# Second graph layer: all parts in float32r, one group's matrices copied by GpSimd, two groups' made by VectorE in one step

## The chip, the cores and the metric

The kernel runs on one core of a Trainium2 chip. The metric is device microseconds for one launch; the time before is the median of three runs. The engines are named as in the profile: PE (TensorE, with PEld for its weight loads), DVE (VectorE), ACT (ScalarE), POOL (GpSimd) and SP, which here only issues DMAs.

## The reference

Four graph layers on 3327 nodes with 512 features, each with a residual around it. Layers 0 to 2 are graph attention with 8, 4 and 8 heads, layer 3 averages neighbours. The change touches layer 1, which has four heads of 128 features:

```python
h = jnp.maximum(_layernorm(x, axis=-1), 0.0)
Wh = (h @ W).reshape(n, 4, 128)
sl = jnp.einsum('nhd,hd->nh', Wh, a_l)
sr = jnp.einsum('nhd,hd->nh', Wh, a_r)
e = leaky_relu(sl[:, :, None] + sr.T[None, :, :], 0.2)
e = where(adj + eye > 0, e, -inf)
alpha = softmax(e, axis=2)
x = x + elu(einsum('nhm,mhd->nhd', alpha, Wh))
```

The exponential of a leaky ReLU of a sum is a product on each side of the kink: where sl + sr > 0 it is exp(sl) exp(sr), elsewhere exp(0.2 sl) exp(0.2 sr). So the softmax sum for one head is two matrix products, one over the neighbours with sl + sr > 0 and one over the other neighbours, with 0/1-like matrices (the mask holds 2.0 for an edge; the factor cancels in the division) and the rows exp(sr) Wh and exp(0.2 sr) Wh, each with the factor itself as a 129th column.

## The kernel before

Nodes lie in 26 tiles of 128. Outputs are worked through in seven chunks (six of four tiles, one of two); sources are grouped as `JG`: three groups of six tiles (0 to 2) and two of four (3 and 4). In `attention`, for each chunk and head of layer 1, there are two halves (`a` = 0 for the positive side, 1 for the other), and for each half passes over pairs of output tiles. A pass runs all 26 source tiles for its two output tiles; both accumulators lie in PSUM (`acc`).

The weights of each matmul are a 128x128 block of the 0/1 matrix. `matrices` makes these in fp8 for all five groups: `compare` asks for sl + sr > 0 (L670 on ACT by a scaled ReLU, or L667 on DVE for the source tiles in `GP_ON_DVE[1]`, tiles 18 to 25, groups 3 and 4), then `split` ANDs the result with the mask as 32-bit words (L674). Between the two halves every matrix is turned into that of the other side in place, by XOR with the mask (L794).

The moving operand is the table `ab`, stored in DRAM per group and loaded again for each head and half (L714, from SP's queue, seven buffers). Its form is set by `KIND`, a letter for each group, "bssvv":

- group 0 ("b"): rows are cut into three bf16 pieces (`pieces`: 387 columns), and the fp8 matrix is itself the weights (L762).
- groups 1 and 2 ("s") and 3 and 4 ("v"): rows are cut into two float32r parts (`parts`: 258 columns), and the fp8 matrix is first copied into float32r for the two output tiles of a pass by `real` (L639): "s" by ACT into `ts` (three buffers), "v" by DVE into `tv` (two buffers). The matmul is L759.

After a pass DVE sums the pieces from PSUM into `R` (L780); after the second half of a head it scales and divides (L802 to L809). Finished chunks go to node stages of the next layer, spread over the following passes by `Hooks`: residual and ELU (L866 to L870, the add L869 on POOL), layer norm (L345 to L357, three small steps L350 to L352 on POOL), projection, scaling (L450) and the pieces for layer 2 (L387 to L397, where L395 is a subtraction on POOL). The order on each engine's queue is written by a scheduler from the program's order and the added order-only dependencies (`after`); each engine then works its queue in order.

The matrices lie in `tht` (ten buffers), the scores of the output tiles, broadcast over partitions, in `s1b` (two buffers, loaded at L682), the mask of a chunk in five `m` tiles out of six buffers (L271). The negated scores of the source tiles are in `L.ns2`, one value a partition for each tile and head.

Of the kernel before, what the change touches and what calls it, by code (L numbers as in the profile page):

```python
# [25 lines left out]
F32 = mybir.dt.float32  # L26
BF16 = mybir.dt.bfloat16
I32 = mybir.dt.int32
U32 = mybir.dt.uint32
FP8 = mybir.dt.float8e4  # L30
F32R = mybir.dt.float32r
# [6 lines left out]
P = 128  # L38
# [4 lines left out]
S2_MAX = 30.0  # L43
S_CLIP = 40.0

GP_ON_DVE = [(5, 12, 19), tuple(range(18, 26)), (4, 9, 14, 19, 24)]


KIND = "bssvv"


@with_exitstack
def tile_gnn(ctx: ExitStack, tc: tile.TileContext, x, adj, W0, a01, W1, al, ar, W2, a2,
# [60 lines left out]
    for l in range(3):  # L114
        H, DA, AO, HW = dims(l)
        if l == 1:
            abd.append([dram.tile([H, 2, P, nj, AO], BF16, name=f"ab{l}_{g}") if KIND[g] == "b" else
                        dram.tile([H, 2, P, nj, 2 * DA], F32, name=f"ab{l}_{g}") for g, (_, nj) in enumerate(JG)])
        else:
            abd.append([dram.tile([H, P, nj, HW], BF16, name=f"ab{l}_{g}") for g, (_, nj) in enumerate(JG)])  # L120
    y1d = [dram.tile([n * P, D], F32, name=f"y1_{c}") for c, (_, n) in enumerate(chunks)]
# [247 lines left out]
    def pieces(L, t, AB, pool, first, behind=None):  # L369

        l = L.l
        g, jj = jwhere[t]
        H, DA, AO, HW = dims(l)

        o, two = (t % 2, 2) if first else (0, 1)
        if o == 0:
            L.pt = pool.tile([P, H, 2, two, AO] if l == 1 else [P, H, two, HW], BF16, name="pt", bufs=3 if first else 2)
        pt = L.pt
        nc.gpsimd.memset(pt[:, :, :, o, 3 * DA:AO] if l == 1 else
                         pt[:, :, o].rearrange("p h (a w) -> p h a w", a=2)[..., 3 * DA:AO], 1.0)  # L380

        def dst(s, a):
            if l == 1:
                return pt[:, :, a, o, s * DA:(s + 1) * DA]
            return pt[:, :, o, a * AO + s * DA:a * AO + (s + 1) * DA]
        r = pool.tile([P, 2, H, DA], F32, name="r", bufs=2 if first else 1)
        sb = nc.vector.tensor_sub(r, AB, high(AB))  # L387
        if behind:
            after(sb, behind)
        for a in range(2):  # L390
            cp = nc.scalar.copy(dst(0, a), high(AB[:, a]))
            if behind:
                after(cp, behind)
        for a in range(2):
            nc.gpsimd.tensor_sub(dst(2, a), r[:, a], high(r[:, a]))  # L395
        for a in range(2):
            nc.scalar.copy(dst(1, a), high(r[:, a]))  # L397
        js = slice(jj + 1 - two, jj + 1)
        if o == two - 1 and l == 1:
            for a in range(2):  # L400
                L.to_store.append((abd[l][g][:, a, :, js, :].rearrange("h p j w -> p h j w"), pt[:, :, a]))
        elif first and o == two - 1:
            if g not in ahead:
                ahead[g] = pieces_tile(L, bp, g)
            nc.sync.dma_start(ahead[g][:, js], pt[:, 0])
            stored[t] = nc.sync.dma_start(abd[l][g][:, :, js, :].rearrange("h p j w -> p h j w"), pt).ins.name
        elif o == two - 1:
            L.to_store.append((abd[l][g][:, :, js, :].rearrange("h p j w -> p h j w"), pt))
# [46 lines left out]
    def parts(L, t, AB, pool, first, behind=None):  # L455

        l = L.l
        g, jj = jwhere[t]
        H, DA, AO, HW = dims(l)
        H2 = H // 2  # L460
        if l == 1 and KIND[g] != "b":
            for f in range(2):
                hs = slice(f * H2, (f + 1) * H2)
                pt = pool.tile([P, H2, 2, 2, DA], F32R, name="pt", bufs=2)
                v = pt.rearrange("p h a s d -> p s a h d")
                cp = nc.scalar.copy(v[:, 0], AB[:, :, hs])
                if behind:
                    after(cp, behind)
                nc.vector.tensor_sub(v[:, 1], AB[:, :, hs], v[:, 0].bitcast(F32))
                L.to_store.append((abd[l][g][hs, :, :, jj, :].rearrange("h a p w -> p h a w"),  # L470
                                   pt.rearrange("p h a s d -> p h a (s d)").bitcast(F32)))
        else:
            pieces(L, t, AB, pool, first, behind)
        if t == JG[g][0] + JG[g][1] - 1:
            js = slice(JG[g][0], t + 1)
            nc.vector.tensor_scalar(L.ks2[:, js], L.s12[:, 1, js, :], BIG, None, op0=ALU.mult)
            nc.vector.tensor_scalar(L.ns2[:, js], L.s12[:, 1, js, :], -1.0, None, op0=ALU.mult)
# [153 lines left out]
            while self.tiles or self.flying:  # L631
                self.run(1, 0, 0)

    def real(a, g, ks, th):

        nj = JG[g][1]
        k0, k1 = ks[0], ks[-1] + 1
        t = mp.tile([P, 2, nj, P], F32R, name="ts" if KIND[g] == "s" else "tv", bufs=3 if KIND[g] == "s" else 2)
        (nc.scalar.copy if KIND[g] == "s" else nc.vector.tensor_copy)(t[:, :k1 - k0, :nj], th[a][g][:, k0:k1])  # L639
        return t  # L640

    ahead = {}
# [42 lines left out]
    def attention(L, hooks, open_next, close):  # L685
# [5 lines left out]
        for c, (t0, nt) in enumerate(chunks):  # L691
# [3 lines left out]
            for h in range(H):  # L695
# [10 lines left out]
                for a in range(2 if l == 1 else 1):  # L706
                    row = []
                    for g, (_, nj) in enumerate(JG):
                        if l == 1:
                            tl = mp.tile([P, JM * 2 * DA], F32R, name="ab", bufs=7)  # L710
                            two = KIND[g] != "b"
                            w = 2 * DA if two else AO
                            v = (tl if two else tl.bitcast(BF16))[:, :nj * w].rearrange("p (j w) -> p j w", j=nj)
                            ld = nc.sync.dma_start(v.bitcast(F32) if two else v, abd[l][g][h, a])  # L714
                        else:
                            if g in ahead:
                                v = ahead.pop(g)
                            else:
                                v = pieces_tile(L, mp if l else bp, g)
                                ld = nc.sync.dma_start(v, abd[l][g][h])  # L720
                        row.append(v)
                    ab.append(row)
# [4 lines left out]
                for g in range(len(JG)):  # L727
                    if g in early:
                        pv, gv = early.pop(g)
                    else:  # L730

                        pt = mp.tile([P, PER * JM * P], FP8, name="tht", bufs=10 if l == 1 else 7)
                        gt = pt if l == 1 else mp.tile([P, PER * JM * P], FP8, name="gt", bufs=7)
                        pv, gv, words, steps = matrices(L, nt, h, g, s1v, masks[g], pt, gt)
                        for step in steps:
                            step()
                        if l == 1:
                            flip.append(words)
                    th[0].append(pv)
                    th[1].append(gv)  # L740
                R = mp.tile([P, PER, 2, DA], F32, name="R", bufs=1)
                deg = l == 0 and h == 0
                for a in range(2 if l == 1 else 1):
# [5 lines left out]
                    for ks, js in passes:  # L749
                        thr = {}  # L750
                        for j in js:
                            g, jj = jwhere[j]
                            if l == 1 and KIND[g] != "b" and g not in thr:
                                thr[g] = real(a, g, ks, th)
                            for k in ks:
                                if j == 0:
                                    acc[k] = accs.tile([P, 512], F32, name="acc")
                                if g in thr:
                                    mm = nc.tensor.matmul(acc[k][:, :2 * DA], thr[g][:, k - ks[0], jj, :], ab[a][g][:, jj, :],  # L759
                                                     start=(j == 0), stop=(j == NT - 1), skip_group_check=True)  # L760
                                elif l == 1:
                                    mm = nc.tensor.matmul(acc[k][:, :3 * DA], th[a][g][:, k, jj, :], ab[a][g][:, jj, :3 * DA],  # L762
                                                     start=(j == 0), stop=(j == NT - 1), skip_group_check=True)
                                else:
                                    o = 1 if deg else 0
# [11 lines left out]
                            continue  # L777
                        for k in ks:
                            if l == 1:
                                nc.vector.tensor_reduce(R[:, k, a, :], acc[k][:, :3 * DA].rearrange("p (s d) -> p d s", s=3),  # L780
                                                        AX.X, ALU.add)
                            else:
                                v = acc[k][:, :2 * AO].rearrange("p (a w) -> p a w", a=2)[:, :, :3 * DA]
                                nc.vector.tensor_reduce(R[:, k], v.rearrange("p a (s d) -> p a d s", s=3), AX.X, ALU.add)  # L784
# [113 lines left out]
    with tc.tile_pool(name="first", bufs=1) as fp:  # L898
# [47 lines left out]
        while hooks.small:  # L946
# [1 line left out]
    A, R = [("A", D, F32, n) for n in A_BUFS], ("R", PER * 2 * 129, F32, 1)  # L948
    ab, gt, tht = ("ab", JM * 400, BF16, 7), ("gt", PER * JM * P, FP8, 7), ("tht", PER * JM * P, FP8, 7)
    tags = [[A[0], ("R", PER * 2 * 65, F32, 1), tht, ("tr", JM * P, BF16, 5), ("abx", 4 * 400, BF16, 4), gt],  # L950
            [A[1], ("ab", JM * 258, F32R, 7), R, ("ts", 2 * JM * P, F32R, 3), ("tv", 2 * 4 * P, F32R, 2), tht[:3] + (10,)],
            [A[2], ab, ("R", PER * 2 * 65, F32, 1), tht, gt]]
    hooks.masks = in_steps([mask_steps(ip, t, g) for t, g in order[20:]])
    for l in range(3):
# [530 lines left out]
```

## Time and profile before

| What | Value |
|---|---|
| Median of three runs | 3552.45 us (3546.64 to 3554.89) |
| Profiled execution, span | 3551.1 us (no other time of this execution is listed) |
| PE busy | 3442.3 us, 97% of the span |
| DVE busy | 2624.3 us, 74% |
| ACT busy | 2507.0 us, 71% |
| POOL busy | 618.8 us, 17% |
| Layer 1, first to last aggregation matmul | 1233.3 to about 2072 us |
| Mean granted TensorE clock | 0.990 |

A row of the groups names the line, engine and operation, the tiles written and read, the shape of what is written and read, and the count; then busy time in all, mean nanoseconds of one, and the idle time of that engine just before, with what ended most of it. A row of the timeline gives the start, the length, and a run of equal instructions with its count. PE's rows of consecutive matmuls overlap, since their ends are modelled; starts are the safer reading.

### The profile page before, as it was taken

Reading aid. Unit: us, or ns where it says so; the run is one execution under the profiler, and the core shown is the slowest. Engines: PE = TensorE matmul, PEld = TensorE weight load, DVE = VectorE, ACT = ScalarE, POOL = GpSimd, SP = SyncE. Lnnn points to the kernel's source line nnn. Section 1 sums busy time; section 2 is a strip of 40 time slices with the busy share of each in tenths; the row PEclk is TensorE's granted clock in tenths of the full one; section 3 lists DMA queues with packets and bytes.
Section 4 is the critical chain, followed back from the end, with each engine's and each line's share of the span. In section 5 each row is a group of like instructions: output and inputs, shape, how many; then the busy total and the mean of one; then the engine's idle time right before and its main releaser. Section 6 shows DMA issues by size and latency. Waiting matters only on the chain. (4 is left out here: it accounts for less than half of the span.)

```text
span 3551.1 us, 77646 instructions
## 1 busy us (share of the span) xinstructions
PE 3442.3 (97%) x30751; PEld 3107.2 (88%) x30751; DVE 2624.3 (74%) x5227; ACT 2507.0 (71%) x4113; POOL 618.8 (17%) x858
## 2 busy tenths in 40 slices
PE   7899999999999999999999989999999999999998
PEld 6789999999999888888888869989898989876887
DVE  7788888888887699888888868867676768672121
ACT  5777787878787789888888677767666757572111
POOL 6611222112111202222223320101010101020000
PEclk9999999999999999999999999999999999999999
DMA  7699999999857787777777875555545555576331
GB/s 207 223 282 251 233 263 238 268 260 250 256 203 247 246 285 276 279 269 273 269 273 254 332 268 190 191 175 189 183 166 181 185 172 188 168 271 257 105 107 54
DMA packets 398120, 797.72 MB, mean 225 GB/s; under 512 B 112970, under 2 KB 221845, under 8 KB 397105
## 3 DMA queue, kind: packets, MB, share of 16 engines
q1 hardware_dynamic: 363890, 723.14, 63.4%
q0 software_dynamic: 28128, 62.42, 7.6%
q10 hardware_dynamic: 5726, 7.08, 0.6%
q8 instruction: 245, 4.01, 0.5%
q14 instruction: 131, 1.07, 0.1%
HBM read 663.59 MB, written 129.64 MB: 223 GB/s over the span
## 5 line engine op out<-in xcount | busy, mean ns | idle before, releaser
L670 ACT ACTIVATE gt<-s1b,ks 128x512 fp8e4<-128x512 f32 (+1 forms) x2448 | 1448.2, 677 | 276.4 <-issue 160.1
L766 PE MATMUL acc<-ab,tht 128*128 128x195 bf16 (+1 forms) x9112 | 1553.1, 248 | 5.4 <-DVE tht L674 4.6
L769 PE MATMUL acc<-ab,gt 128*128 128x195 bf16 (+1 forms) x9112 | 1552.2, 248 | 5.0 <-DVE rc L806 3.3
L769 PEld LDWEIGHTS <-gt 128*128 128x128 fp8e4 x10744 | 1053.6, 98 | 40.1 <-issue 27.4
L766 PEld LDWEIGHTS <-tht 128*128 128x128 fp8e4 x10744 | 1053.4, 98 | 24.8 <-DVE tht L674 11.5
L674 DVE TENSOR_TENSOR tht<-gt,m 128x768 uint32<-128x768 uint32 (+3 forms) x557 | 445.5, 800 | 129.4 <-ACT gt L670 125.5
L676 DVE TENSOR_TENSOR gt<-tht,m 128x768 uint32<-128x768 uint32 (+3 forms) x557 | 448.0, 805 | 8.7
L639 ACT CAST ts<-tht 128x1536 fp32r<-128x1536 fp8e4 x208 | 300.0, 1470 | 55.6 <-PE acc L759 52.5
L759 PE MATMUL acc<-ab,ts 128*128 128x258 f32 x2496 | 333.4, 289 | 4.7 <-ACT ts L639 3.4
L759 PEld LDWEIGHTS acc<-ab,ts 128*128 128x128 f32 x2496 | 313.2, 190 | 13.2 <-ACT ts L639 3.8
L667 DVE TENSOR_SCALAR gt<-s1b,ns 128x512 fp8e4<-128x512 f32 (+1 forms) x446 | 218.2, 495 | 129.4 <-PE acc L769 125.1
L1021 PE MATMUL acc<-y,mf 128*128 128x512 f32 x1352 | 309.8, 391 | 1.1 <-DVE mf L1016 1.1
L670 ACT ACTIVATE tht<-s1b,ks 128x512 fp8e4<-128x512 f32 (+1 forms) x504 | 308.4, 680 | 2.3 <-DMA s1b<-s 1.7
L1021 PEld LDWEIGHTS acc<-y,mf 128*128 128x128 f32 x1352 | 253.6, 188 | 57.2 <-DVE mf L1016 1.5
L769 PE MATMUL acc<-abx,gt 128*128 128x195 bf16 (+1 forms) x1632 | 287.4, 249 | 11.6 <-DVE rc L806 5.6
L766 PE MATMUL acc<-abx,tht 128*128 128x195 bf16 (+1 forms) x1632 | 287.8, 249 | 4.6 <-DVE tht L674 3.0
L869 POOL TENSOR_TENSOR xt<-xt,e 128x512 f32<-128x512 f32 x72 | 121.9, 1693 | 916.8 <-DVE e L868 583.9
L784 DVE TENSOR_REDUCE R<-acc 128x130 f32<-128x390 f32 x416 | 214.2, 554 | 79.5 <-PE acc L769 78.9
L762 PE MATMUL acc<-ab,tht 128*128 128x387 bf16 x1248 | 225.8, 329 | 8.9 <-DMA ab<-ab 5.8
L1018 ACT CAST mf<-m 128x768 fp32r<-128x768 fp8e4 (+1 forms) x78 | 59.1, 762 | 244.5 <-PE acc L1021 232.7
L759 PE MATMUL acc<-ab,tv 128*128 128x258 f32 x1664 | 218.8, 283 | 1.4 <-DVE tv L639 1.2
L759 PEld LDWEIGHTS acc<-ab,tv 128*128 128x128 f32 x1664 | 207.2, 189 | 2.9 <-DVE tv L639 2.1
(163 smaller groups left out, 3710.2 us busy)
## 6 DMA issues: line engine op xcount, KB each, us to landing
ab<-ab SPq DMA_DIRECT2D x333, 600.0 KB, 5.3
ab<-ab SPq DMA_DIRECT2D x112, 774.0 KB, 6.5
ab<-ab SPq DMA_DIRECT2D x112, 516.0 KB, 5.3
ab<-ab SPq DMA_DIRECT2D x112, 400.0 KB, 4.0
abx<-ab SPq DMA_DIRECT2D x110, 400.0 KB, 7.9
ab<-ab SPq DMA_DIRECT2D x56, 582.0 KB, 7.3
s1b<-s SPq DMA_DIRECT2D x120, 256.0 KB, 6.5
m<-mask SPq DMA_DIRECT2D x69, 384.0 KB, 4.4
```

The source lines that it names most:

```text
L639: (nc.scalar.copy if KIND[g] == "s" else nc.vector.tensor_copy)(t[:, :k1 - k0, :nj], th[a][g][:, k0:k1])
L667: nc.vector.tensor_scalar(gv[:, :, jj, :], s1v, L.ns2[:, j, h:h + 1], 2.0, op0=ALU.is_gt, op1=ALU.mult, saturate=False)
L670: nc.scalar.activation(gv[:, :, jj, :], s1v, AF.Relu, bias=L.ks2[:, j, h:h + 1], scale=BIG, saturate=False)
L674: nc.vector.tensor_tensor(pu, gu, mu, ALU.bitwise_and)
L676: nc.vector.tensor_tensor(gu, pu, mu, ALU.bitwise_xor)
L759: mm = nc.tensor.matmul(acc[k][:, :2 * DA], thr[g][:, k - ks[0], jj, :], ab[a][g][:, jj, :], start=(j == 0), stop=(j == NT - 1), skip_grou ...
L762: mm = nc.tensor.matmul(acc[k][:, :3 * DA], th[a][g][:, k, jj, :], ab[a][g][:, jj, :3 * DA], start=(j == 0), stop=(j == NT - 1), skip_grou ...
L766: nc.tensor.matmul(acc[k][:, :3 * DA + o], th[0][g][:, k, jj, :], ab[0][g][:, jj, :3 * DA + o], start=(j == 0), stop=False, skip_group_che ...
L769: mm = nc.tensor.matmul(acc[k][:, AO:AO + 3 * DA + o], th[1][g][:, k, jj, :], ab[0][g][:, jj, AO:AO + 3 * DA + o], start=False, stop=(j == ...
L784: nc.vector.tensor_reduce(R[:, k], v.rearrange("p a (s d) -> p a d s", s=3), AX.X, ALU.add)
L869: nc.gpsimd.tensor_add(xt, xt, e)
L1021: nc.tensor.matmul(acc[k], mf[:, jj, :], y2[g][:, jj, s, :], start=(j0 + jj == 0 and s == 0), stop=(j0 + jj == NT - 1 and s == 1))
```

## The change

`KIND` becomes "gssdd", and all five groups are stored and loaded as two float32r parts of 258 columns. What follows from the letters:

- group 0 ("g"): `real` copies its fp8 matrix into float32r with GpSimd (`tg`, two buffers), and the matmul is that of the other groups.
- groups 1 and 2 ("s"): unchanged.
- groups 3 and 4 ("d"): no fp8 matrix is made; there is no compare, AND, XOR or copy. For each pass and source tile, one DVE instruction compares the broadcast scores with the tile's negated score (greater for the first half, less or equal for the second), multiplies by the mask and writes float32r (`td`, two buffers).

`GP_ON_DVE[1]` is empty, since its tiles are those of groups 3 and 4. The reduce from PSUM sums two parts of 129. The `ab` tiles get two names, `ab6` (five buffers) and `ab4` (three), and `tht` goes from ten buffers to seven. The branches for group 0's bf16 pieces in `pieces`, `parts`, the tables in DRAM and the matmuls go.

```diff
-GP_ON_DVE = [(5, 12, 19), tuple(range(18, 26)), (4, 9, 14, 19, 24)]
+GP_ON_DVE = [(5, 12, 19), (), (4, 9, 14, 19, 24)]
-KIND = "bssvv"
+KIND = "gssdd"
+TD = 2
...
-        if l == 1 and KIND[g] != "b":
+        if l == 1:
             for f in range(2):
...
-    def real(a, g, ks, th):
+    def real(L, a, g, ks, th, h, s1v, mask):
-        nj = JG[g][1]
+        j0, nj = JG[g]
         k0, k1 = ks[0], ks[-1] + 1
-        t = mp.tile([P, 2, nj, P], F32R, name="ts" if KIND[g] == "s" else "tv", bufs=3 if KIND[g] == "s" else 2)
-        (nc.scalar.copy if KIND[g] == "s" else nc.vector.tensor_copy)(t[:, :k1 - k0, :nj], th[a][g][:, k0:k1])
+        if KIND[g] == "d":
+            t = mp.tile([P, 2, nj, P], F32R, name="td", bufs=TD)
+            for jj in range(nj):
+                nc.vector.scalar_tensor_tensor(t[:, :k1 - k0, jj, :], s1v[:, k0:k1, :], L.ns2[:, j0 + jj, h:h + 1],
+                                               mask[:, k0:k1, jj, :], op0=ALU.is_le if a else ALU.is_gt, op1=ALU.mult)
+            return t
+        copy = {"g": nc.gpsimd.tensor_copy, "s": nc.scalar.copy}[KIND[g]]
+        t = mp.tile([P, 2, nj, P], F32R, name="t" + KIND[g], bufs=3 if KIND[g] == "s" else 2)
+        copy(t[:, :k1 - k0, :nj], th[a][g][:, k0:k1])
         return t
...
-                            tl = mp.tile([P, JM * 2 * DA], F32R, name="ab", bufs=7)
-                            two = KIND[g] != "b"
-                            w = 2 * DA if two else AO
-                            v = (tl if two else tl.bitcast(BF16))[:, :nj * w].rearrange("p (j w) -> p j w", j=nj)
-                            ld = nc.sync.dma_start(v.bitcast(F32) if two else v, abd[l][g][h, a])
+                            v = mp.tile([P, nj, 2 * DA], F32R, name=f"ab{nj}", bufs=5 if nj == JM else 3)
+                            ld = nc.sync.dma_start(v.bitcast(F32), abd[l][g][h, a])
...
                     if g in early:
                         pv, gv = early.pop(g)
+                    elif l == 1 and KIND[g] == "d":
+                        pv = gv = None
...
-                        pt = mp.tile([P, PER * JM * P], FP8, name="tht", bufs=10 if l == 1 else 7)
+                        pt = mp.tile([P, PER * JM * P], FP8, name="tht", bufs=7)
...
-                            if l == 1 and KIND[g] != "b" and g not in thr:
-                                thr[g] = real(a, g, ks, th)
+                            if l == 1 and g not in thr:
+                                thr[g] = real(L, a, g, ks, th, h, s1v, masks[g])
...
-                                elif l == 1:
-                                    mm = nc.tensor.matmul(acc[k][:, :3 * DA], th[a][g][:, k, jj, :], ab[a][g][:, jj, :3 * DA],
-                                                     start=(j == 0), stop=(j == NT - 1), skip_group_check=True)
...
-                                nc.vector.tensor_reduce(R[:, k, a, :], acc[k][:, :3 * DA].rearrange("p (s d) -> p d s", s=3),
+                                nc.vector.tensor_reduce(R[:, k, a, :], acc[k][:, :2 * DA].rearrange("p (s d) -> p d s", s=2),
                                                         AX.X, ALU.add)
```

More of the change, by code (lines that the diff above doesn't have):

```diff
@@ L116, in tile_gnn @@
         if l == 1:
-            abd.append([dram.tile([H, 2, P, nj, AO], BF16, name=f"ab{l}_{g}") if KIND[g] == "b" else
-                        dram.tile([H, 2, P, nj, 2 * DA], F32, name=f"ab{l}_{g}") for g, (_, nj) in enumerate(JG)])
+            abd.append([dram.tile([H, 2, P, nj, 2 * DA], F32, name=f"ab{l}_{g}") for g, (_, nj) in enumerate(JG)])
         else:
@@ L376, in pieces @@
         if o == 0:
-            L.pt = pool.tile([P, H, 2, two, AO] if l == 1 else [P, H, two, HW], BF16, name="pt", bufs=3 if first else 2)
+            L.pt = pool.tile([P, H, two, HW], BF16, name="pt", bufs=3 if first else 2)
         pt = L.pt
-        nc.gpsimd.memset(pt[:, :, :, o, 3 * DA:AO] if l == 1 else
-                         pt[:, :, o].rearrange("p h (a w) -> p h a w", a=2)[..., 3 * DA:AO], 1.0)
+        nc.gpsimd.memset(pt[:, :, o].rearrange("p h (a w) -> p h a w", a=2)[..., 3 * DA:AO], 1.0)
         def dst(s, a):
-            if l == 1:
-                return pt[:, :, a, o, s * DA:(s + 1) * DA]
             return pt[:, :, o, a * AO + s * DA:a * AO + (s + 1) * DA]
@@ L398, in pieces @@
         js = slice(jj + 1 - two, jj + 1)
[L399 to L402, printed above, removed]
+        if first and o == two - 1:
             if g not in ahead:
@@ L950, in tile_gnn @@
     tags = [[A[0], ("R", PER * 2 * 65, F32, 1), tht, ("tr", JM * P, BF16, 5), ("abx", 4 * 400, BF16, 4), gt],
-            [A[1], ("ab", JM * 258, F32R, 7), R, ("ts", 2 * JM * P, F32R, 3), ("tv", 2 * 4 * P, F32R, 2), tht[:3] + (10,)],
+            [A[1], ("ab6", JM * 258, F32R, 5), ("ab4", 4 * 258, F32R, 3), R, ("ts", 2 * JM * P, F32R, 3),
+             ("tg", 2 * JM * P, F32R, 2), ("td", 2 * 4 * P, F32R, TD), tht],
             [A[2], ab, ("R", PER * 2 * 65, F32, 1), tht, gt]]
```

## The prediction

> **What bounds the kernel now.** I read the page's busy shares first (PE 97%), then busy time by stretch, to find the second layer: its first aggregation matmul starts at 1233 us and its last ends near 2072 us.
>
> ```profile
> 1233.00:2072.00 839.00, 822.82 (x5936) 718.07 (x5937) 729.25 (x1373) 705.43 (x964) 205.50 (x231) 0.99 0.78 279
> ```
>
> The columns are the length, then busy time of PE, PEld, DVE, ACT and POOL, the granted clock, the DMA share and GB/s. PE has 823 of 839 us and bounds the layer, but DVE has 729 (87%) and ACT 705 (84%): any PE gain stops at the next engine soon. The timeline of PE gives the price of one pass (two output tiles against all 26 source tiles):
>
> ```profile
> 1280.93 2.15 PE L762 MATMUL acc<-ab,tht 128*128 128x387 bf16 x12
> 1282.78 3.19 PE L759 MATMUL acc<-ab,ts 128*128 128x258 f32 x24
> 1285.80 2.08 PE L759 MATMUL acc<-ab,tv 128*128 128x258 f32 x16
> 1287.72 2.15 PE L762 MATMUL acc<-ab,tht 128*128 128x387 bf16 x12
> ```
>
> Start to start, 12 bf16 matmuls take 1.85 us (0.154 each) and 40 float32r ones 4.94 us (0.1235 each); a pass takes 6.79 us. There are 2496/24 = 104 passes (the first ones of the layer are cut in two). The groups of DVE inside that stretch:
>
> ```profile
> L639 DVE CAST tv<-tht 128x1024 fp32r<-128x1024 fp8e4 x208 | 145.9, 702 | 55.1 <-PE acc L759 55.1
> L780 DVE TENSOR_REDUCE R<-acc 128x129 f32<-128x387 f32 x206 | 104.9, 550 | 6.2 <-PE acc L759 5.4
> L667 DVE TENSOR_SCALAR tht<-s1b,ns 128x512 fp8e4<-128x512 f32 x192 | 93.8, 536 | 0.9 <-PE acc L762 0.9
> L674 DVE TENSOR_TENSOR tht<-tht,m 128x512 uint32<-128x512 uint32 x48 | 34.9, 728 | 0.7 <-DMA m<-mask 0.2
> L804 DVE TENSOR_TENSOR R<-R 128x516 f32<-128x516 f32 x24 | 17.3, 721 | 0.0
> ```
>
> Consecutive DVE instructions overlap by about 0.08 us (in the timeline a 0.68 us cast is followed 0.60 us later), so I price each by its step from start to start. The last view decides: POOL and DVE in the same microseconds, twice.
>
> ```profile
> 1493.67 4.60 POOL L869 TENSOR_TENSOR xt<-xt,e 128x512 f32<-128x512 f32 x1 [1.30 <-DVE e L868]
> ...
> 1493.52 2.14 DVE L794 TENSOR_TENSOR tht<-tht,m 128x768 uint32<-128x768 uint32 x3
> 1495.59 0.94 DVE L674 TENSOR_TENSOR tht<-tht,m 128x768 uint32<-128x768 uint32 x1
> 1496.46 0.68 DVE L639 CAST tv<-tht 128x1024 fp32r<-128x1024 fp8e4 x1
> 1497.06 1.01 DVE L780 TENSOR_REDUCE R<-acc 128x129 f32<-128x387 f32 x2
> ```
>
> ```profile
> 1459.51 2.07 POOL L395 TENSOR_TENSOR pt<-r 128x520 bf16<-128x520 f32 x2 [15.22 <-DVE r L387]
> ...
> 1459.35 2.51 DVE L809 TENSOR_SCALAR A<-R,rc 128x128 f32<-128x128 f32 x4
> ```
>
> In the first, a POOL add that takes 1.26 us elsewhere lasts 4.60: it stands still through five DVE instructions and ends with the reduces, which read PSUM. In the second, four DVE multiplications of 0.28 us (four take 0.87 us at 1284.78) need 2.51 us while POOL runs two subtractions. The two engines shut each other out, except where DVE reads PSUM.
>
> **PE.** Six of 26 tiles change from 387-column bf16 to 258-column float32r: 12 x (0.154 - 0.1235) = 0.37 us a pass, 38 us over 104 passes. PE then needs 839 - 38 = 801 us for the layer.
>
> **DVE, removed.** 208 casts tv at a step of 0.60: 125 us. 224 compares (192 of 512 elements at 0.395, 32 of 256 at 0.26): 84. The masking (L674) and the flip (L794) of the two four-tile groups, 96 x 0.60 + 16 x 0.34: 63. The reduce reads 258 columns for 387: 129 x 1.04 ns (the slope between L804's 260 and 516 elements, 0.34 to 0.606 us in steps) x 208 = 28. Sum 300.
>
> **DVE, added.** Changed `real` issues four scalar_tensor_tensor of 2x128 elements for each of two groups in each of 104 passes: 832. L804 at 260 elements has a step of 0.34; a scalar read per partition costs 0.06 more (L1030 with it 0.751 us, L1031 without 0.692). I take 0.40: 333 us; the low end is 0.34, 283 us. Without contention DVE stands at 729 - 300 + 333 = 762 us, below PE's 801.
>
> **POOL, added.** 104 copies of 2x6x128 fp8 into float32r. No row shows one. POOL's own start costs 0.2 us (L283's 32 words: 0.199 at least); L869 then takes 2.08 ns an element with two float32 operands, L395 1.64 with a bf16 result. Upper end 0.2 + 1536 x 2.08 = 3.4 us; lower end half of L395's rate, 1.45 us. A copy reads one operand for L869's two, which gives 1.8; I take 2.0, as fp8 must be widened too. That is 208 us beside the 206 that POOL has: no bound of its own, and with two buffers it may run a pass ahead.
>
> **What a copy costs DVE.** In this layer I compared every DVE instruction with the median of its form: together 35 us longer, against 72 POOL additions and subtractions of 1.05 to 1.26 us (80 us undisturbed), so 0.44 of POOL's time is lost. That is the low end. The high end is a copy minus what of it falls under the pair of PSUM reduces, d - 0.4, since almost all else on DVE now has two SBUF operands. For d = 2.0: 0.9 to 1.6 us, I take 1.3, as after the change DVE is fuller and copies are longer than the reduces: 135 us. DVE becomes the bound at 762 + 135 = 897 us. Of its 110 idle us now, 55 are waits for PE to free a tv buffer and vanish; I keep 30 for head, tail and waits for ACT. Layer: 927 against 839, +88 us.
>
> The Trainium skill, SBUF — State Buffer, section Who interferes with whom, says that a DVE instruction with two SBUF inputs and a GpSimd one that reads SBUF exclude each other, the second blocking for the whole of the first. The 4.60 us row agrees; the average of 0.44 is milder. By the rule taken whole, each copy would cost DVE its 2.0 us: 208 instead of 135, and the layer would be 161 us longer instead of 88. The skill's GPSIMD Engine Reference, section 3.1, gives 1.03 to 1.8 cycles an element at 1.2 GHz for one-input loops, an estimated 1.5 to 2.5 us a copy with L283's start; no run here shows one yet.
>
> **Other edits.** ACT keeps its 504 compares and 208 casts. The parts of tiles 0 to 5 are made while the first layer runs: two ACT copies, the wide subtraction and two POOL subtractions fewer for six tiles, one DVE subtraction more; PE covers them there (862 of 875 us from 340 to 1215); uncovered, at most 6 x 2 x 0.65 = 8 us. The loads of group 0 grow from 582 to 774 KB, 56 of them: 11 MB in a layer that moves 279 GB/s at a DMA share of 0.78, hidden; uncovered 6.5 us for one. On SP, the next heads' s1b and the next chunk's masks now wait for the last scalar_tensor_tensor instead of an earlier compare or flip, and ab loads queue behind them; a mask lands in 4.4 us, so at most 6 chunks x 4.4 = 26 us, hidden while DVE is late anyway. The flip of group 0 on DVE now waits for POOL's copy, with all later DVE work behind it; this is inside the 1.3. On POOL, copies stand behind the adds (L869, there L866) that wait for e and x rows; cover is the second tg buffer, one pass, and a miss stops PE at the head of a pass.
>
> **Sum.** The profile spans 3551.1 us; nothing else of that execution's time is listed, and the three runs' median is 3552.45, 1.4 above. 3552 + 88 = 3640 us.
>
> **Rivals.**
> - *PE's gain arrives.* If a copy costs DVE 0.64 us (d = 1.45, 0.44 of it) and the fused step is 0.34, DVE needs 729 - 300 + 283 + 66 = 778, under PE's 801: 3552 - 38 = 3514; with some 15 us of stalls 3529. It decides where copies cost less than (801 - 762)/104 = 0.38 us at my step, 0.86 at the low step. For it: POOL was idle three quarters of the layer, and PSUM reduces leave room. Against: the pairs above. Chance 0.15.
> - *The same within 0.2%*: low d with step 0.40, DVE 762 + 66 = 828 and 10 us idle: 3552 on the line. Chance 0.05.
> - *Copies as slow as L869.* d = 3.4 and a loss of 3.0: 762 + 312 + 30 = 1104, 3817 us. Speaks for it: POOL widens fp8 in a loop no row shows. Chance 0.15.
> - *POOL starves* behind unbroken runs of eight fused instructions (8 x 0.40 = 3.2 us, as in the 4.60 us row) and PE waits for tg. The reduces come once a pass and open the gate, and the second buffer covers one pass; if half the copies still came 3.2 us late, PE would need 801 + 52 x 3.2 = 967, 3680 us. Chance 0.15.
>
> My case has 0.50, with its own range 3575 to 3700. The range for 8 in 10 is 3535 to 3770: below it lies most of the first rival, above it most of the slow copies. A measurement tells 0.2%, 7 us, from no change: faster 0.15, same 0.05, slower 0.80.
>
> **What would show it.** Right: DVE busy above 93% of a layer of 900 us or more; POOL copies of about 2 us; PE waiting for td and tg for some 80 us in all, where DVE's tv wait for PE is gone; fused instructions that mostly last 0.48 us and sometimes 2. Wrong: copies under 1.5 us, fused instructions that hardly stretch, PE still full, a pass of 6.4 us.

## The result: 2.3% slower, nearly all of it in the second layer

The changed kernel takes 3633.7 us (median of four runs, 3630.1 to 3635.2) against 3553.5: a ratio of 1.0227, with a 95% interval of 1.0213 to 1.0242. The forecast was 3640 us in a range of 3535 to 3770, so sign and size hold. Its span is 3630.8 us against 3551.1. From its first to its last aggregation matmul the second layer takes 911 us (1239.0 to 2150.1) against 839: 72 of the 80 us. It starts 6 us later than before and ends 78 us later; what follows it takes 2 us longer.

Busy time by stretch of the changed kernel; columns as in the prediction (length, PE, PEld, DVE, ACT, POOL, granted clock, DMA share, GB/s):

```profile
1233.00:2152.00 919.00, 833.63 (x5948) 785.13 (x5948) 839.21 (x1655) 706.03 (x964) 355.64 (x335) 0.95 0.75 267
1400.00:1960.00 560.00, 518.38 (x3735) 490.46 (x3734) 526.80 (x1022) 443.27 (x589) 226.52 (x214) 0.97 0.73 261
```

The same interior stretch of the kernel before:

```profile
1400.00:1960.00 560.00, 556.99 (x4063) 489.58 (x4063) 490.26 (x896) 481.94 (x650) 152.16 (x162) 1.00 0.77 271
```

Away from head and tail, the bound has changed sides: PE was busy 99.5% and DVE 88%; now DVE has 94% and PE 93%, at a granted clock of 0.97 for 1.00. The timeline of PE shows a pass of the changed kernel in which nothing waits:

```profile
1266.33 1.61 PE L759 MATMUL acc<-ab,tg 128*128 128x258 f32 x12
1267.77 3.06 PE L759 MATMUL acc<-ab,ts 128*128 128x258 f32 x24
1270.67 2.07 PE L759 MATMUL acc<-ab,td 128*128 128x258 f32 x16
```

The twelve matmuls of group 0 take 1.44 us from start to start, for 1.85; with the next pass starting about 1272.7 it takes 6.35 us for 6.79. PE's gain is there, some 46 us over 104 passes, and it is lost to waits and to the clock: PE pauses 84 us in the layer for 15 before, and its busy time has not fallen (826 us for 823), with 67 us of it at half the granted clock, for 10 before. Who made PE wait, in the changed kernel's layer (in all, times, longest):

```profile
PE acc L759 <- POOL tg L640: 26.2, 13, 9.5
PE acc L759 <- DVE td L635: 25.3, 31, 2.2
PE acc L759 <- ACT ts L640: 23.9, 14, 3.6
```

The waits name three makers of matrices, but ACT and POOL wait for DVE's ANDs (L675) and flips (L791) in their turn, POOL 101 and 71 us (its row below), ACT:

```profile
ACT ts L640 <- DVE tht L675: 51.4, 24, 6.4
ACT ts L640 <- DVE tht L791: 46.4, 23, 8.0
```

The groups of the changed kernel's layer:

```profile
L635 DVE SCALAR_TENSOR_TENSOR td<-s1b,ns,m 128x256 fp32r<-128x256 f32 x824 | 448.4, 594 | 41.7 <-PE acc L759 38.9 <-DMA s1b<-s 2.5
L777 DVE TENSOR_REDUCE R<-acc 128x129 f32<-128x258 f32 x208 | 77.7, 413 | 4.9 <-PE acc L759 4.8
...
L640 POOL CAST tg<-tht 128x1536 fp32r<-128x1536 fp8e4 x104 | 177.6, 1717 | 303.7 <-PE acc L759 114.4 <-DVE tht L675 100.6 <-DVE tht L791 71.0
```

Half of the fused instructions last 0.473 us or less, but the mean is 0.594: 111 of them last over 0.7 us. The reduces, which read PSUM, are as short as their size says. The reason is in the timeline, POOL and then DVE in the same microseconds:

```profile
1669.29 3.19 POOL L640 CAST tg<-tht 128x1536 fp32r<-128x1536 fp8e4 x2 [3.78 <-DVE tht L675]
...
1669.07 3.69 DVE L635 SCALAR_TENSOR_TENSOR td<-s1b,ns,m 128x256 fp32r<-128x256 f32 x3
1672.68 0.74 DVE L777 TENSOR_REDUCE R<-acc 128x129 f32<-128x258 f32 x2
```

During two copies DVE gets three fused instructions done, in 3.69 us where three take 1.27 elsewhere. It is so over the whole layer: the 92 fused instructions that ran beside a copy lasted 1.11 us in the mean, the 517 that ran beside no POOL instruction 0.473, and 56 PSUM reduces beside a copy 0.413, as always.

### The profile page after: what moved, and what is told of

It reads as the page before. It is cut to its first block, busy times and chain, and to the rows that moved or that the text cites. A ratio compares the mean times of both kernels' runs of the same rounds, so it can differ in the third digit from the quotient of the medians.

```text
span 3630.8 us, 78098 instructions
## 1 busy us (share of the span) xinstructions
PE 3450.1 (95%) x30751; PEld 3171.9 (87%) x30751; DVE 2728.8 (75%) x5521; ACT 2501.4 (69%) x4101; POOL 763.0 (21%) x944
## 5 line engine op out<-in xcount | busy, mean ns | idle before, releaser
L675 DVE TENSOR_TENSOR tht<-gt,m 128x768 uint32<-128x768 uint32 (+3 forms) x557 | 445.2, 800 | 130.2 <-ACT gt L671 127.1
L635 DVE SCALAR_TENSOR_TENSOR td<-s1b,ns,m 128x256 fp32r<-128x256 f32 x832 | 451.8, 593 | 41.7 <-PE acc L759 38.9
L866 POOL TENSOR_TENSOR xt<-xt,e 128x512 f32<-128x512 f32 x72 | 111.7, 1552 | 860.5 <-DVE e L865 639.8
L759 PE MATMUL acc<-ab,td 128*128 128x258 f32 x1664 | 258.9, 299 | 30.8 <-DVE td L635 25.3
L759 PEld LDWEIGHTS acc<-ab,td 128*128 128x128 f32 x1664 | 226.7, 196 | 50.1 <-DVE td L635 40.4
L640 POOL CAST tg<-tht 128x1536 fp32r<-128x1536 fp8e4 x104 | 177.6, 1717 | 303.7 <-PE acc L759 114.4
```

Of the source, the lines that this page charges most:

```text
L635: nc.vector.scalar_tensor_tensor(t[:, :k1 - k0, jj, :], s1v[:, k0:k1, :], L.ns2[:, j0 + jj, h:h + 1], mask[:, k0:k1, jj, :], op0=ALU.is_le ...
L640: copy(t[:, :k1 - k0, :nj], th[a][g][:, k0:k1])
L675: nc.vector.tensor_tensor(pu, gu, mu, ALU.bitwise_and)
L866: nc.gpsimd.tensor_add(xt, xt, e)
```

## The experiments

Three measures recur, all over the layer, from its first to its last aggregation matmul, and all from one profiled execution of each kernel. *Excess* is how much longer VectorE's instructions lasted than the medians of their forms in the same run. *Gaps* are the pauses of PE of over 0.2 us. *Half clock* is the time at which TensorE was granted half its clock. All three are in us. Ratios are to the kernel before on the same chip.

| Kernel | Ratio, 95% | Layer us | DVE busy | Excess | Gaps | Half clock us |
|---|---|---|---|---|---|---|
| before | 1 | 839 | 729 | 35 | 15 | 10 |
| changed | 1.0227 (1.0213 to 1.0242) | 911 | 834 | 122 | 84 | 79 |
| e1 memset for the copy | 1.0031 (1.0019 to 1.0043) | 851 | 770 | 62 | 50 | 31 |
| e2 copy on VectorE | 1.0176 (1.0158 to 1.0194) | 896 | 851 | 49 | 79 | 68 |
| e3 fused step alone | 1.0088 (1.0070 to 1.0106) | 866 | 783 | 38 | 27 | 24 |
| e4 copy twice | 1.0516 (1.0493 to 1.0539) | 1013 | 941 | 226 | 147 | 157 |
| e5 e3, three score buffers | 1.0066 (1.0050 to 1.0083) | 854 | 788 | 48 | 21 | 7 |
| e6 e3, four td buffers | 1.0086 (1.0069 to 1.0103) | 865 | 786 | 43 | 30 | 27 |
| e7 GpSimd copy alone | 1.0157 (1.0140 to 1.0174) | 883 | 790 | 134 | 79 | 72 |
| e8 copy in six pieces | 1.0194 (1.0171 to 1.0216) | 909 | 825 | 108 | 72 | 65 |
| e9 three td buffers | 1.0215 (1.0188 to 1.0243) | 907 | 848 | 138 | 97 | 68 |
| e10 casts on VectorE, nothing fused | 1.0009 (0.9997 to 1.0021) | 839 | 792 | 48 | 51 | 48 |

### e1: a memset in the copy's place

```diff
-        copy(t[:, :k1 - k0, :nj], th[a][g][:, k0:k1])
+        if KIND[g] == "g":
+            nc.gpsimd.memset(t[:, :k1 - k0, :nj].bitcast(F32), 2.0)
+            copy(t[:, :1, :1, :8], th[a][g][:, k0:k0 + 1, :1, :8])
+        else:
+            copy(t[:, :k1 - k0, :nj], th[a][g][:, k0:k1])
```

> Group 0's float32r matrix is filled by a GpSimd memset of the same 1536 elements, which reads nothing, and only 8 elements of it are then copied from the fp8 matrix, so GpSimd still waits for VectorE's AND and flip, and VectorE's flip for GpSimd. Left out: group 0's real matrix (it is 2.0 almost everywhere). Theory (GpSimd's reads shut out VectorE's two-operand instructions): in the changed kernel VectorE's instructions of the layer lasted 123 us beyond the medians of their forms, 88 us more than before; this falls back to 35 to 55 us, the mean fused instruction from 593 to under 500 ns, the layer from 918 us to 805 to 840, the time to 3520 to 3555 us. Rival (the second layer is longer because the copies come late out of GpSimd's queue): a memset of 1.6 us keeps the queue as full, time stays at 3615 us or more. Rival (832 small fused instructions are too slow by themselves): time stays above 3600 us.

It took 3567 us, and the ratio falls from 1.0227 to 1.0031: about 70 of the 80 us are gone. Every figure moved the way the theory said and none as far: 3520 to 3555 us was expected, and for the layer 805 to 840 where it took 851. POOL was as busy in the layer as with the copies (364 us for 353). Its groups and DVE's fused one in this run:

```profile
L641 POOL MEMSET tg<- 128x1536 f32 x104 | 143.8, 1383 | 227.8 <-PE acc L763 227.6
...
L642 POOL CAST tg<-tht 128x8 fp32r<-128x8 fp8e4 x104 | 41.5, 408 | 82.1 <-DVE tht L679 46.6 <-DVE tht L795 30.0 <-DVE s L427 2.9
...
L635 DVE SCALAR_TENSOR_TENSOR td<-s1b,ns,m 128x256 fp32r<-128x256 f32 x824 | 389.9, 523 | 34.8 <-PE acc L763 34.5 <-DMA s1b<-s 0.2
```

POOL still waits for AND and flip (47 and 30 us), yet the mean fused instruction fell from 0.594 to 0.523 us and the excess by half. The 129 fused instructions that ran beside a memset and nothing else on POOL lasted 0.473 us in the mean, as if alone. So it is the copies' reading of SBUF that lengthens them, not POOL's time: both rivals, at 3600 us or more, fall. The excess stayed above the 35 to 55 expected; 104 small copies and POOL's other work still read. In one respect e1 leaves out more than the reading: the memset need not wait for the AND, so a matrix is ready one small copy after the AND or flip, not one whole copy. What part of the 70 us that is, e1 doesn't tell.

### e2: group 0's copy on VectorE

```diff
-        copy = {"g": nc.gpsimd.tensor_copy, "s": nc.scalar.copy}[KIND[g]]
+        copy = {"g": nc.vector.tensor_copy, "s": nc.scalar.copy}[KIND[g]]
```

> Group 0's copy is made by VectorE instead of GpSimd, all else as in the changed kernel. Theory (the copies cost VectorE about as much as if it made them): 104 casts of 1536 elements at a step of (768+64)/0.96 = 0.87 us add 90 us to VectorE where the lock took 88, so VectorE's busy time stays near 840 us and the time at 3620 to 3650 us, while the excess over the medians falls to about 35 us. Rival (late copies in GpSimd's queue): the 26 us of TensorE's waits for the copy vanish, time 3590 to 3610 us.

3617.8 us lies between the two ranges. Nearly as the theory said, the excess falls to 49 us (about 35 was expected) and DVE's busy time stays, 851 us for 834. The same interior stretch in this run:

```profile
1400.00:1960.00 560.00, 523.29 (x3834) 495.86 (x3833) 552.20 (x1115) 455.28 (x606) 136.68 (x153) 0.98 0.76 267
```

DVE is at 98.6%. Moving 104 casts off DVE to POOL gave back their 90 us, and took 73 in excess and 33 in idle time: the move lengthens the layer by some 15 us.

### e3, e5 and e6: the fused step alone

From the kernel before: `KIND = "bssdd"`, `GP_ON_DVE[1]` empty, the fused branch of `real`, seven fp8 buffers. e5 gives the scores three buffers, e6 gives td four:

```diff
# e5
-        s1b = rp.tile([P, WMAX], F32, name="s1b", bufs=2)
+        s1b = mp.tile([P, WMAX], F32, name="s1c", bufs=3) if l == 1 else rp.tile([P, WMAX], F32, name="s1b", bufs=2)
# e6
-            t = mp.tile([P, 2, nj, P], F32R, name="td", bufs=2)
+            t = mp.tile([P, 2, nj, P], F32R, name="td", bufs=4)
```

> The kernel before with one part of the change: groups 3 and 4 made by VectorE in one fused step; group 0 stays bf16 with its fp8 matrix as weights, so nothing is added to GpSimd. Theory: VectorE needs 729 - 272 + 333 = 790 us, TensorE keeps its 823 and bounds the layer; 3545 to 3565 us. Rival (832 small fused instructions make the matrices late by themselves): 3575 us or more, with TensorE waiting over 40 us for them.

> As the kernel without the GpSimd group (group 0 in bf16, groups 3 and 4 fused), with three buffers for the broadcast scores in the second layer instead of two. That kernel took 1.0088 of the time before, 27 us more in the second layer, half of it in the last chunk (100 against 86 us). Theory: the fused step holds a head's scores to its last pass, so ScalarE's compares of the head after next start too late; a third buffer takes 15 to 25 us back, time 3555 to 3568 us, last chunk under 92 us. Rival (VectorE waits in its queue for a td buffer, and the ANDs behind it come late): no change, 3575 to 3590 us.

> The same kernel with two buffers for the scores again, and four td buffers instead of two. Rival (waits for a td buffer, 54 us of VectorE's idle time there): VectorE runs a pass ahead, these waits fall under 20 us, time 3555 to 3568 us. Theory (scores held too long): the waits may fall, but the time stays at 3575 to 3590 us.

e3 took 3583.4 us, outside the theory's range, and not by the rival's way either: PE waited 2.6 us for td. DVE needed 783 us, near the 790 computed, but the layer grew by 27. Half of it lies in the last chunk of two output tiles, 100.0 us for 86.4. e5 brought that chunk to 89.7, but the run only to 3576.3, and its interval overlaps e3's: the held scores explain at most a part. (The profiled execution of e5, and so its row in the table, is its fastest, 3565 us.) e6 removed DVE's waits for td (54 us) and left the time as it was (3583.5), as its theory had it; its last chunk took 92.7 us with two score buffers, so that chunk alone doesn't decide for the held scores. What the other 20 us are was not settled.

### e4: the copy made twice

```diff
         copy(t[:, :k1 - k0, :nj], th[a][g][:, k0:k1])
+        if KIND[g] == "g":
+            copy(t[:, :k1 - k0, :nj], th[a][g][:, k0:k1])
```

> Each GpSimd copy of group 0 is made twice into the same tile, all else as in the changed kernel. Theory: the excess of VectorE's instructions grows by another 80 to 130 us (0.85 to 1.25 us a copy), the layer by 80 to 150 us, time 3715 to 3785 us. Rival (only the wait for the first matrices of a pass matters, with two buffers as cover): under 3690 us.

3736.4 us (two runs), inside the theory's range: 104 more copies add 105 us of excess, 1.0 us each, and 102 us to the layer. The waits of PE in this run:

```profile
PE acc L761 <- DVE td L635: 83.9, 83, 2.9
PE acc L761 <- POOL tg L642: 35.3, 9, 11.1
PE acc L761 <- ACT ts L640: 14.7, 12, 1.7
```

The growth is in the waits for td, which POOL doesn't make (84 us for 25), more than for the copy itself (35 for 26).

### e7 and e10: the two float32r halves without the fused step

`KIND = "gssvv"` with the separate compare, mask and cast of groups 3 and 4; the fp8 buffers become five of six tiles and three of four, to fit. e10 is e7 with one word changed:

```diff
-        copy = {"g": nc.gpsimd.tensor_copy, "s": nc.scalar.copy, "v": nc.vector.tensor_copy}[KIND[g]]
+        copy = {"g": nc.vector.tensor_copy, "s": nc.scalar.copy, "v": nc.vector.tensor_copy}[KIND[g]]
```

> The other half of the change alone: group 0 in float32r, copied by GpSimd; groups 3 and 4 compared, masked and cast by VectorE as before; fp8 matrices in five buffers of six tiles and three of four, to fit. Theory: VectorE without excess needs 694 - 28 = 666 us, the copies cost it 0.7 us each (73 us, between the excess of the changed kernel and that of the casts on VectorE) beside the 35 of before, 774 us, under TensorE's 785 to 800; the layer takes 800 to 830 us and the time is 3510 to 3545 us, faster than before. Rival (a GpSimd copy at the head of every pass stops TensorE whatever VectorE has to do): waits for tg of 25 us or more, 3555 us or more.

> All five groups in float32r as after the change, with no GpSimd copy and no fused step: VectorE casts groups 0, 3 and 4 from fp8. VectorE needs 694 - 28 + 90 = 756 us and the 35 to 50 us of excess of before; TensorE needs 785. If the shared port was the loss, the layer is 830 to 850 us and the time 3540 to 3562 us, about that of before. If a matrix made just in time for every group is a loss by itself, 3575 us or more.

I missed e7 by far: 3608.7 us, not 3510 to 3545, with a layer of 883 us, not 800 to 830. The excess grew to 134 us, 0.95 a copy against before, for the 0.7 I had taken, but that is only 26 us: DVE's busy time, 790 us, is near the 774 expected. The rest is idle time: DVE's is 94 us, where the expectation left it 26 to 56. The rival's reason fails too: PE waited 8.7 us for tg. Its waits in this run, and DVE's casts:

```profile
PE acc L763 <- DVE tv L640: 41.6, 33, 3.4
PE acc L763 <- ACT ts L640: 13.1, 10, 3.3
PE acc L763 <- POOL tg L640: 8.7, 2, 6.6
...
L640 DVE CAST tv<-tht 128x1024 fp32r<-128x1024 fp8e4 x206 | 168.5, 822 | 37.4 <-PE acc L763 37.4
```

DVE's own casts, 0.822 us in the mean in this run for 0.702 before, came too late for PE (42 us), and DVE in turn waited for PE to free their buffers (37 us). e10 is as it was foretold: 3560.2 us, no different from before (1.0009). So float32r for group 0 pays for 104 casts of 0.95 us on DVE and no more.

e7 and e10 also show what a sum of DVE's work leaves out. DVE is equally busy in both (790 and 792 us), yet the layer takes 883 us with the copies on GpSimd and 839 without: DVE idles 94 us for 47. The copies cost idle time beside the time by which they lengthen instructions.

Taken together, with group 0 by GpSimd or VectorE and groups 3 and 4 fused or separate, the four times are 3634 and 3618 fused, 3609 and 3560 separate. The fused step costs 58 us where DVE also makes group 0's casts: DVE's busy time rises by 60, and by the prices used, 333 - 272 = 61 was due. The copies on GpSimd cost 49 us where nothing is fused. Together they cost 74, less than the sum. The ratios, each against its own chip, say nearly the same (59, 53 and 77 us). The fp8 buffers differ too, seven of one size where the step is fused and five and three where it is separate; no pair of runs has one fused, one separate and the same buffers.

### e8 and e9: is VectorE stopped at the wrong moment, or too long in all?

```diff
# e8
-        copy(t[:, :k1 - k0, :nj], th[a][g][:, k0:k1])
+        for jj in range(nj) if KIND[g] == "g" else (slice(0, nj),):
+            copy(t[:, :k1 - k0, jj], th[a][g][:, k0:k1, jj])
# e9
-TD = 2
+TD = 3
-                        pt = mp.tile([P, PER * JM * P], FP8, name="tht", bufs=7)
+                        pt = mp.tile([P, PER * JM * P], FP8, name="tht", bufs=5 if l == 1 else 7)
```

> The changed kernel with each GpSimd copy cut into six copies of 256 elements, one for each source tile. Same elements, six starts of about 0.2 us for one: GpSimd's copying grows from 178 to 230 us or more. If what counts is that VectorE is stopped for 1.5 us at a stretch at the wrong moment (its busy time is only 91% of the layer), pieces of 0.4 us let it in between: long fused instructions (over 0.7 us) go, TensorE's waits for td fall from 25 to under 12 us, time 3600 to 3620 us. If what counts is GpSimd's total time on the shared port, the excess stays at 120 us or grows, and the time is 3630 us or more.

> The changed kernel with three td buffers instead of two, and five fp8 buffers instead of seven to make room. If a blocked VectorE only comes late, a third buffer lets it work ahead: TensorE's waits for td fall from 25 to under 12 us and the time to 3605 to 3622 us. If VectorE's capacity is the bound, the waits move to tg and ts and the time stays at 3625 to 3645 us.

e8 took 3625.7 us, between its two ranges, and e9 3630.9, in the second of its own, with intervals that overlap the changed kernel's. Pieces of 0.40 us halve the long fused instructions (61 for 111), but the excess is 108 us and PE's waits for td are 23. A third buffer leaves these waits at 24, where they were to move to tg and ts; DVE's idle time falls from 77 to 59 us and its excess rises to 138. So neither shorter stops nor more room is worth more than some 12 us; in e9 what DVE gains in idle time it loses in excess. (e9 also has two fp8 buffers fewer.)

e8 shows one thing more. At their medians the pieces keep GpSimd busy 250 us where whole copies take 163, and the excess did not grow. The loss fits the number of elements read, which is the same, better than the length of the instructions.

## Why the prediction was right

The sum was DVE's: 762 us uncontended, 135 for the copies, 30 idle, 927. Measured: 834 busy, of which 87 is growth of excess over before, leaves 747; idle 77; 911. The mechanism holds: copies that read SBUF lengthen DVE's two-operand instructions (e1), twice the copies cost about twice (e4), and with the same casts on DVE and nothing fused the kernel is as fast as before (e10). But two terms were mis-sized, one 48 us too high and one 47 too low. That they cancelled is luck, and so is how near 3640 came to 3634.

- *PE's gain*, 0.37 us a pass: measured 0.44. It is real, and e10 shows what it buys: 104 casts on DVE.
- *DVE's price of the edit*: the fused step was right (0.396 from start to start for 0.40, 0.473 us long for 0.48), and DVE's total without the copies' share is 15 us under mine. One reading behind it doesn't hold: L1030 has not only a scalar operand that L1031 lacks, it also reads PSUM, so the 0.06 us is not shown to be the scalar's.
- *The copy*: 1.46 us undisturbed and 1.57 in the median, for the 2.0 I took; the low end, half of L395's rate, came nearest.
- *A copy's cost to DVE*, 1.3 us, was the first mis-sized term: 0.83 in the changed kernel, 1.0 in e4, 0.95 in e7. Against the copy's median of 1.57 that is a share of 0.53 to 0.64, between the low end of 0.44 and the high one, all but 0.4 us, which is 0.75. In the changed kernel 74 of the 87 us fall on instructions that ran beside a copy, 0.71 us a copy; nearly all the rest falls beside POOL's adds and subtractions. The Trainium skill, SBUF — State Buffer, section Who interferes with whom, has the mechanism as e1 shows it: only a GpSimd instruction that reads SBUF gets in the way of a two-operand DVE instruction. Its rule taken whole would be 1.57 us a copy; no run here shows that much.
- *Idle time*, 30 us, was the second: it is 77, half of it waits for a td buffer (38.9 us), which I said would vanish with PE's lead. Both engines idle, PE in 65 pauses. DVE is the bound in the interior, at 94%, not over the whole layer at 91.5%. That part of this comes with the copies, e7 against e10 shows; why, in what order of waits, stays open.
- *The rival that PE's gain arrives* fails at its own condition: copies cost more than 0.38 us. *Starving* shows as 9.5 us once, in the last chunk, and in 12 shorter waits for tg (17 us), not in every second pass. *Slow copies* did not occur.
- *Other edits*: the held scores, which I priced together with the masks at up to 26 us and called hidden, are a candidate for part of the 27 us by which e3's layer grew; the rest of that is open.

Of the signs named ahead, a layer of over 900 us was seen, and fused instructions that mostly last 0.48 us and sometimes 2 (46 of 832 over 1.5). DVE is busy 91.5% of the layer, under the 93% named. Copies of 1.57 us in the median are nearer to the 1.5 that was to prove me wrong than to the 2 that was to prove me right, and an undisturbed pass takes 6.35 us, though the mean pass takes 8.8. PE's waits for td and tg are 52 us, not 80; those for ACT, 24 us, I had not named.

## What to carry to other kernels

An instruction moved from VectorE to GpSimd is not off VectorE while both read SBUF and VectorE is nearly full: these copies of 1.57 us cost it half to two thirds of their length, and idle time besides. Compare that with what VectorE needs for the same work (here 0.87 us for 0.8 to 1.0). For short pieces the share is smaller (0.29 in e8, for the same elements). Fusing cheap steps into one saves nothing if the fused form costs more an element and covers fewer columns at a time: here a fused instruction of 256 elements takes 0.396 us from start to start, as much as a separate compare of 512. Add up steps from start to start before fusing. When the engine behind the bound is at 87%, a change that unloads the bound by 5% and loads that engine has to be summed on that engine.

## What the runs showed of the hardware

- GpSimd's widening copy of 1536 fp8 elements takes 1.46 us undisturbed: with the 0.2 us of its smallest instruction, 0.82 ns an element. Six pieces take 0.39 to 0.40 each.
- A GpSimd memset of the same size, which reads nothing, left VectorE's two-operand instructions alone (e1: 0.473 us beside it, 0.474 beside nothing). It did lengthen TENSOR_SCALAR from SBUF to SBUF: three of these beside nothing but a memset lost 2.2 us together, few as they are.
- VectorE's reduces from PSUM lasted no longer beside a copy (56 of them, 0.413 us).
- PE's waits have a second price: the granted clock falls to half in stretches of 3.4 us or a multiple of it, 17 times and 79 us in the changed layer, 3 times and 10 us in that of before, 157 us in e4. PE was busy in 67 of the 79 us, so about half of that, 34 us of PE's work, was lost; no run shows how much of it reached the time. The Trainium skill, TensorE: Matmul & The Clock Gate, Part 1, ties this to an idle window of about 3.4 us; here only two gaps of PE were longer than that, and in the 3.4 us before each of the 17 stretches PE had paused 1.1 to 2.8 us in all.
